# A deformable convolution and a mixture of convolutions on one core: later offset sorting, and other engines for a few copies

## The chip, the core and the metric

The kernel runs on one core of a Trainium2 chip. The metric is the device time of one execution in microseconds. The engines are TensorE (PE; its weight loads are shown as PEld), VectorE (DVE), ScalarE (ACT), GpSimd (POOL) and SyncE (SP). SP, ACT and POOL also issue DMAs; a name with a q (SPq, ACTq) stands for the part of an engine that issues and waits. Each engine takes its instructions in the order in which the program lists them.

## What is computed

The input x has 8 images of 128 channels and 64 x 64 pixels. There are two layers, each of which adds to x. Cut to what matters:

```
gn(v)   : normalise over each group of 4 channels and all pixels of an image
# layer 0: deformable 3 x 3 convolution, then batch norm over all images, ReLU
om      = conv3x3(gn(x), off_w) + off_b          # 27 channels: 9 dy, 9 dx, 9 mask
val[k]  = bilinear sample of gn(x) at (pixel + tap k + (dy, dx)[k]) * sigmoid(mask[k])
y       = sum over k of w[k] applied to val[k] + b
x       = x + relu(batchnorm(y) * gamma + beta)
# layer 1: four expert convolutions, two chosen per image by a gate, and a shared one
x       = x + conv3x3(gn(x), sum of gated experts + shared) + biases
```

The batch norm needs y of all eight images, so layer 1 starts only after layer 0 has done the last one.

## The kernel before

**Sampling as matmuls.** All offsets are below 2 in size (the kernel counts them and has a general path that is not entered here). So a sample is a weighted sum over an 8 x 8 pixel patch. An image is cut into 8 bands of 8 rows, and a band into 15 column tiles, which overlap. For each tile the pixels must stand as patch position by channel. This is the tile `xt`.

- `pick` (VectorE, L768) gathers the 8 even tiles of a band into `picked`, `pixels` has TensorE turn them (L785) in two rounds of four, and ScalarE evicts them (L790).
- `share` (L802) makes the 7 odd tiles from the even ones by eight DMAs of 56 KB within SBUF, because an odd tile is made of the halves of its two even neighbours.

**Weights.** A sample's weights are a product of a y part and an x part with a tent shape. They come from two tables in DRAM for each image, `taby` and `tabx`. For each band, GpSimd issues eight loads of the y part (`load_y`, L719, 90 KB each) and two of the x part (`load_x`, L734, 576 KB each). `spread` turns distances into tents (ScalarE L753 and L756, VectorE L759). `weights` (L825, VectorE) multiplies both into `s`.

**Band loop.** It runs over 64 bands and one more turn. In turn g the five groups of band g are sampled first (`sample`: TensorE L841, eviction ScalarE L851), with `weights` three groups ahead. Then `conv(g - 1)` runs the nine taps of the band before as matmuls on the samples (L890, eviction L898, store of y by SP, L900). Between the taps, by number, stand the preparations for later bands: taps 0 and 1 turn the pixels of band g + 2, tap 2 issues `load_x(g + 3)`, tap 3 issues `share(g + 2)` on SP, tap 4 picks band g + 3, taps 1, 3, 5 and 7 hold the halves of `spread(g + 2)`.

**Tables of the next image.** A generator, `tables(b)`, holds the work that makes the tables of image b, cut into steps. The band loop calls for three steps after each tap (`tick`). A `pause(n)` lets n steps go by, so it says how far along the band loop the next instructions are put. The order in `tables(b)` is:

1. mean and variance by group: matmul pm (L316), d, e, gm on VectorE (L319 to L323), matmul pv (L326), ve (L331), a power on GpSimd (L334), then the normalisation of the image in place
2. the offset convolution, as sums on VectorE (L369, or L419 and L421) and matmuls (L388 or L454), into `om`
3. `om` is stored twice to DRAM, by rows and by columns (L521, L528)
4. both are loaded again, sorted by row (L565, ten DMAs) and by column (L551, five DMAs) into `combo`
5. `distances_y` on VectorE (L608 to L614), sigmoids of the mask (ScalarE L655), then five tents (L633, L637) multiplied by the mask (L670); between the second and the third come L608 again and `distances_x` (L623) and the stores of the x table (L588)
6. the store of the y table (L660)

Between the column loads and step 5 stands the pause that the change touches:

```python
for k, *where in by_column:
    turned_in(nc.sync if b or k == 0 else nc.gpsimd, k, *where)
yield from pause((50, 9)[b] if b < 2 else 17)
```

For images 2 to 7, `tables(b)` starts in image b - 2, in its band 5, and its last steps fall into bands 2 to 4 of image b - 1.

**The start.** Image 0 has no bands to hide behind. Its `tables(0)` runs through before the loop. On the way it picks and turns bands 0 and 1, and near its end, after the first rows of the y table are stored (L660, five DMAs), it issues `share(0)` and `share(1)` on ACT's queue, and two of band 0's eight y loads behind them. Then `tables(1)` is run up to the power on GpSimd, and `dw_sb`, the weights of the taps, is scaled by -1 (L948). Only then come the first three products of `weights`, two on VectorE and one on GpSimd, and the loads of bands 1 and 2.

**Order of the work.** It is written out by hand, there is no scheduler. The DMAs that SP issues get eight completion semaphores in turn: one is not issued before the one eight places earlier has landed.

Of the kernel before, what the change touches and what calls it, by code (L numbers as in the profile page):

```python
# [8 lines left out]
F32 = mybir.dt.float32  # L9
I32 = mybir.dt.int32  # L10
AF = mybir.ActivationFunctionType
# [5 lines left out]
P = 128  # L17
# [24 lines left out]
T = 4  # L42
Q = T + 2 * REACH
HALF = Q * Q
NCOL = 15
# [4 lines left out]
EVEN = (NCOL + 1) // 2  # L50
# [7 lines left out]
BLOCK = "block"  # L58
# [7 lines left out]
def deform_moe_conv(  # L66
# [18 lines left out]
    nc = tc.nc  # L85
# [94 lines left out]
    def dense():  # L180

        with ExitStack() as st:
            st.enter_context(tc.manual_schedule())
            a1 = st.enter_context(tc.tile_pool(name="d1", bufs=1))
# [7 lines left out]


            picked = [a1.tile([P, EVEN, 2, Q, Q], F32, name=f"picked{i}") for i in range(2)]
            for t in pads:
                nc.gpsimd.memset(t[:, 0:ROWPAD], 0.0)
                nc.gpsimd.memset(t[:, ROWPAD + H :], 0.0)
# [11 lines left out]
            ident = a1.tile([P, P], F32, name="ident")  # L209
# [22 lines left out]
            for i, base, mask in ((0, T - REACH, T - 1), (1, 0, Q - 1), (2, T, Q - 1)):  # L232
                one = place_i[:, i : i + 1]
# [36 lines left out]
            def pause(n):  # L270
                for _ in range(n):
                    yield
# [34 lines left out]
            def tables(b):  # L307
# [224 lines left out]
                if b == 0:  # L532
                    for g in range(2):
                        pick(g)
                        for _ in pixels(g):
                            pass
                    pick(2)
                nc.vector.tensor_reduce(
                    most[:, b : b + 1], omr, AX.X, ALU.max, apply_absolute_value=True
                )  # L540
# [30 lines left out]
                    yield from pause(27)  # L571
                for k, *where in by_column:
                    turned_in(nc.sync if b or k == 0 else nc.gpsimd, k, *where)
                yield from pause((50, 9)[b] if b < 2 else 17)

                def moved(side, t, *dims):

# [119 lines left out]
                for i in (3, 0, 4, 1, 2):  # L697
                    masked(i)
                    store_y(i, 1, soon)
                for g in range(2):  # L700
                    share(g, nc.scalar)
                for k in range(2 * T):
                    load_y(0, k, (nc.sync, nc.gpsimd, nc.scalar, nc.gpsimd)[k % 4])
                for _ in statistics(1):
# [7 lines left out]
            def load_y(g, k, engine):  # L712

                if g >= len(bands):
                    return
                b, j = bands[g]
                h, r = divmod(k, T)
                at = HALF * h + r * Q
                engine.dma_start(  # L719
                    out=y_wts[g % 2][at : at + NR * Q, r].rearrange("p a b c -> p (a b c)"),  # L720
                    in_=bass.AP(
                        tensor=y_table[b].tensor,
                        offset=y_table[b].offset + (2 * T * j + k) * GROW,
                        ap=[[YSTEP, NR], [0, Q], [1, YSTEP]],
                    ),
                )
# [34 lines left out]
            def pick(g):  # L761

                if g >= len(bands):
                    return
                b, j = bands[g]
                for h in range(2):
                    one = pads[b % 2][:, 2 * T * j + T * h : 2 * T * j + T * h + 1, 0:1]
                    nc.vector.tensor_copy(  # L768
                        picked[g % 2][:, :, h],
                        bass.AP(  # L770
                            tensor=one.tensor, offset=one.offset,
                            ap=[list(one.ap[0]), [Q, EVEN], [W, Q], [1, Q]],
                        ),
                    )


            def pixels(g):

                if g >= len(bands):
                    return  # L780
                xts[g] = a2.tile([P, NCOL, P], F32, name="xt")
                for c0 in range(0, EVEN, 4):
                    pt = ps_c.tile([P, 4, P], F32, name="pt", tag="pc")
                    for c in range(4):
                        nc.tensor.transpose(  # L785
                            pt[:, c],
                            picked[g % 2][:, c0 + c].rearrange("p h y x -> p (h y x)"),
                            ident,
                        )
                    nc.scalar.copy(xts[g][:, c0 : c0 + 4], pt)  # L790
                    yield


# [1 line left out]
            def share(g, engine):  # L795

                if g >= len(bands):
                    return
                for x0 in range(T):
                    for side in range(2):  # L800
                        rows = slice(x0 + T * side, P, Q)
                        engine.dma_start(  # L802
                            out=xts[g][rows, EVEN:].rearrange("p c n -> p (c n)"),
                            in_=xts[g][rows, 1 - side : EVEN - side].rearrange("p c n -> p (c n)"),
                        )
# [134 lines left out]
                pass  # L940
            for _ in made:
                pass
            for _ in range(2):
                while next(later) != BLOCK:
                    pass
            for _ in range(8):
                next(later)
            nc.scalar.activation(dw_sb, dw_sb, AF.Copy, scale=-1.0)  # L948
            AHEAD = 3
            for n in range(AHEAD):  # L950
                weights(n, nc.vector if n < AHEAD - 1 else nc.gpsimd)
# [33 lines left out]
            for g in range(len(bands) + 1):  # L985
                b, j = bands[g] if g < len(bands) else (B, 0)
                if j == NB - 3:
                    means_of = statistics(b + 2)
                turned = pixels(g + 2)
                if j == NB - 2:  # L990
                    tick()
                for q in range(NGR):
                    if g < len(bands):
                        if g or q + AHEAD < NGR:
                            weights(g * NGR + q + AHEAD)
                        sample(g * NGR + q)
                        if q in (2, 3):
                            for k in range(T * (q - 2), T * (q - 1)):
                                load_y(g + 2, k, nc.gpsimd)
                    if q == 1:  # L1000
                        put_off()
                taps = conv(g - 1) if g else iter(())
                twice = 2 if g and bands[g - 1][1] == NB - 1 else 1
                for done, _ in enumerate(taps):
                    part, odd = divmod(done, twice)
                    if odd == 0 and part in PIXELS:
                        next(turned, None)
                    if odd == 0 and part == 2:
                        load_x(g + 3, nc.gpsimd)
                    if odd == 0 and part in SPREAD:  # L1010
                        step, half = divmod(SPREAD.index(part), 2)
                        if step:
                            spread(g + 2, HALVES[half], ())
                        else:
                            spread(g + 2, sides_=(half,), clip=False)
                    if odd == 0 and part == 3:
                        share(g + 2, nc.sync)
                    if odd == 0 and j == NB - 3 and part in (0, 1, 2, 4):
                        for _ in range(2):
                            next(means_of, None)  # L1020
                    if odd == 0 and j == NB - 3 and part == 7 and b + 2 < B:
                        for _ in made:
                            pass
                        asked, made = True, tables(b + 2)
                        next(made)
                    if odd == 0 and part in BLOCKS and asked:
                        asked = False
                        tick()
                    for _ in range(3 + (g < NB) if twice == 1 else 1 + done % 2):
                        tick()  # L1030
                    if odd == 0 and part == 4:
                        pick(g + 3)
                        if 2 <= j < 5:
                            load_quarter(b + 2, j - 1)
                    if odd == 0 and part == 8 and j == 1:
                        load_quarter(b + 2, 0)
                for _ in turned:
                    pass
                if g == 0:
                    share(2, nc.sync)  # L1040
                    load_x(3, nc.gpsimd)
                    pick(3)
                    spread(1)
                    for n in range(AHEAD):
                        weights(NGR + n)
                    spread(2)
                if g == 4:
                    quad_weights()
                if g < len(bands):
                    late.append((close, g))  # L1050
                xts.pop(g - 1, None)
                if j == 1 and b:
                    nc.vector.bn_aggr(ymvs[:, b - 1], ystats[:, b - 1])
                if (b, j) == (B - 1, 1):
                    reach()
# [596 lines left out]
```

## Time and profile before

| what | us |
|---|---|
| median of 3 runs | 1505.06 (1503.42 to 1509.43) |
| the profiled execution | 1515.66 |
| its span, first to last instruction | 1513.9 |
| first sampling matmul (L841) | 83.55 |
| TensorE busy | 1311.9 |
| VectorE busy | 960.6 |
| ScalarE busy | 784.5 |
| GpSimd busy | 442.2 |

The mean granted clock of TensorE is 0.935 of the full one. Each image takes about 129 us in the middle of layer 0 (its last band's taps start at 514.36 us for image 2 and at 643.09 us for image 3). The sampling ends at about 1140 us, then layer 1 follows.

The profile's page gives busy times, a chain of waits that ended last, and groups of instructions by line. The timeline shows instructions in order of time with the idle time of the engine before each. A stall of TensorE in this kernel is read in three steps: find the gap, see which engine released it, and see in that engine's own timeline what it had stood at.

### The profile page before, as it was taken

What the parts mean: (1) busy time and instruction counts of PE and PEld (TensorE: products, weight loads), DVE (VectorE), ACT (ScalarE), POOL (GpSimd) and SP (SyncE); (2) the same over time, 40 slices, a digit from 0 to 9 for tenths busy, and PEclk for the clock granted to TensorE, in tenths of its full rate; (3) what the DMA queues carried; (4) which work ended last, traced back from release to release, by engine and by line L of the source; (5) the groups of instructions that cost most, each with busy time, mean ns of one, the idle gap of its engine ahead of it and who ended that gap; (6) DMA issues with size and microseconds to landing.
All of it is one profiled execution on the core that took longest, in us unless ns stands there. A gap on an engine that the chain in (4) does not pass through costs nothing.

```text
span 1513.9 us, 22086 instructions
## 1 busy us (share of the span) xinstructions
PE 1311.9 (87%) x7554; PEld 751.2 (50%) x7554; DVE 960.6 (63%) x1985; ACT 784.5 (52%) x1055; POOL 442.2 (29%) x751
## 2 busy tenths in 40 slices
PE   4049788889979997997998899798994999999998
PEld 1033455655645664564665556466652444444443
DVE  5436477548746855864784786544427888888872
ACT  2144674666657675665757566664634232323320
POOL 6242332333324242343433434343403000110100
PEclk9569989989989998998999899899996999999999
DMA  4476774898689788779969987798927345555411
GB/s 144 107 150 161 177 180 110 184 233 205 164 197 219 180 190 210 196 175 210 218 167 196 222 209 182 169 216 205 236 62 230 90 133 162 166 165 155 111 43 58
DMA packets 136670, 256.71 MB, mean 170 GB/s; under 512 B 81554, under 2 KB 84782, under 8 KB 127862
## 3 DMA queue, kind: packets, MB, share of 16 engines
q0 software_dynamic: 55344, 137.45, 41.6%
q1 hardware_dynamic: 80532, 116.45, 27.4%
q10 hardware_dynamic: 674, 1.32, 0.3%
q8 instruction: 62, 1.02, 0.3%
q14 instruction: 58, 0.48, 0.1%
HBM read 180.23 MB, written 45.35 MB: 149 GB/s over the span
## 4 chain that ended last, share of the span: by engine, by line
PE 47%; DMA 24%; DVE 12%; issue 8%; SPq 4%; ACT 3%; POOL 2%; DVEq 0%; POOLq 0%; ACTq 0%
PE pc L1564 17%; PE py L890 15%; PE pq L841 9%; DMA xt<-xt 7%; DMA xwts<-tabx 4%; DMA combo<-colwise 3%; DMA combo<-rowwise 3%; DMA pad<-in_x_dram 3%; PE pc L454 2%; PE pt L785 2%; DMA ywts<-taby 2%; SPq L565 2%; DVE combo L421 2%; DVE s L825 2%; DVE xwts L759 1%
## 5 line engine op out<-in xcount | busy, mean ns | idle before, releaser
L890 PE MATMUL py<-samples,dw_sb 128*128 128x512 f32 (+3 forms) x1296 | 556.4, 564 | 8.0 <-ACT y L898 6.2
L719 POOL DMA_DIRECT2D ywts<-taby x508 | 295.7, 607 | 557.0 <-DVE s L825 483.8
L841 PE MATMUL pq<-s,xt 64*128 64x144 f32 (+1 forms) x3840 | 303.2, 313 | 94.0 <-DVE s L825 67.9
L841 PEld LDWEIGHTS pq<-s,xt 64*128 64x128 f32 x3840 | 273.0, 201 | 139.4 <-issue 97.5
L851 ACT COPY samples<-pq 128x864 f32<-128x864 f32 (+1 forms) x320 | 284.7, 972 | 109.9 <-PE pq L841 108.8
L890 PEld LDWEIGHTS py<-samples,dw_sb 128*128 128x128 f32 x1296 | 230.3, 191 | 208.6 <-issue 179.0
L825 DVE TENSOR_TENSOR s<-xwts,ywts 128x72 f32<-128x72 f32 (+1 forms) x447 | 199.5, 499 | 73.6 <-PE pq L841 65.6
L759 DVE TENSOR_SCALAR xwts<-xwts 128x1152 f32<-128x1152 f32 (+2 forms) x128 | 92.5, 755 | 175.3 <-ACT xwts L753 134.0
L1564 PE MATMUL pc<-v,u 128*128 128x512 f32 x384 | 175.7, 604 | 6.6 <-DVE v L1471 6.4
L1564 PE MATMUL pc<-v,wmix 128*128 128x512 f32 x384 | 173.1, 596 | 0.0
L753 ACT ACTIVATE xwts<-xwts,place 128x1152 f32<-128x1152 f32 (+3 forms) x132 | 152.9, 1162 | 31.0 <-DMA xwts<-tabx 31.0
L1542 ACT ACTIVATE t<-pc,bmix 128x512 f32<-128x512 f32 x32 | 22.0, 687 | 188.9 <-PE pc L1564 100.3
L1564 PEld LDWEIGHTS pc<-v,u 128*128 128x128 f32 x384 | 72.4, 192 | 94.3 <-issue 84.2
L1564 PEld LDWEIGHTS pc<-v,wmix 128*128 128x128 f32 x384 | 71.9, 189 | 90.6 <-issue 88.7
L790 ACT COPY xt<-pt 128x512 f32<-128x512 f32 x128 | 74.8, 584 | 62.6 <-PE pt L785 56.1
L898 ACT ACTIVATE y<-py,db_sb 128x512 f32<-128x512 f32 (+3 forms) x72 | 45.7, 635 | 116.0 <-PE py L890 72.3
L785 PEld LDWEIGHTS pt<-ident,picked 128*128 128x128 f32 x512 | 60.2, 142 | 77.3 <-ACT xt L790 39.8
L734 POOL DMA_DIRECT2D xwts<-tabx x128 | 75.0, 597 | 71.4 <-DMA ywts<-taby 31.9
L785 PE MATMUL pt<-ident,picked 128*128 128x128 f32 x512 | 80.5, 280 | 5.1 <-ACT xt L790 3.1
L670 DVE TENSOR_TENSOR work<-work,combo 64x576 f32<-64x576 f32 x40 | 29.6, 749 | 68.1 <-ACT work L637 68.1
L976 DVE BATCH_NORM_STATS2 ystats<-y 128x6 f32<-128x512 f32 (+3 forms) x72 | 44.4, 625 | 20.0 <-ACT y L898 20.0
L768 DVE COPY picked<-pad 128x512 f32<-128x512 f32 x128 | 48.3, 419 | 1.5 <-PE pt L785 1.5
(200 smaller groups left out, 1070.8 us busy)
## 6 DMA issues: line engine op xcount, KB each, us to landing
xwts<-tabx POOLq DMA_DIRECT2D x128, 576.0 KB, 8.7
ywts<-taby POOLq DMA_DIRECT2D x508, 90.0 KB, 5.4
xt<-xt SPq DMA_DIRECT2D x496, 56.0 KB
pad<-in_x_dram SPq DMA_DIRECT2D x36, 512.0 KB
out_dram<-yo SPq DMA_DIRECT2D x32, 512.0 KB
yd<-y SPq DMA_DIRECT2D x48, 256.0 KB
pad<-yd SPq DMA_DIRECT2D x16, 512.0 KB
x<-yd SPq DMA_DIRECT2D x16, 512.0 KB
```

The lines of the kernel that those rows point to most:

```text
L719: engine.dma_start(out=y_wts[g % 2][at : at + NR * Q, r].rearrange("p a b c -> p (a b c)"), in_=bass.AP(tensor=y_table[b].tensor, offset=y ...
L734: engine.dma_start(out=x_wts[g % 3][HALF * h : HALF * h + HALF], in_=bass.AP(tensor=x_table[b].tensor, offset=x_table[b].offset + (2 * j + ...
L753: nc.scalar.activation(some, some, AF.Abs, bias=columns[side])
L759: nc.vector.tensor_scalar(some, some, -1.0, 0.0, ALU.add, ALU.min)
L768: nc.vector.tensor_copy(picked[g % 2][:, :, h], bass.AP(tensor=one.tensor, offset=one.offset, ap=[list(one.ap[0]), [Q, EVEN], [W, Q], [1, Q]],
L785: nc.tensor.transpose(pt[:, c], picked[g % 2][:, c0 + c].rearrange("p h y x -> p (h y x)"), ident,)
L790: nc.scalar.copy(xts[g][:, c0 : c0 + 4], pt)
L825: engine.tensor_tensor(s[:, :, 3 * at : 3 * (at + k)].rearrange("p m (c x) -> p m c x", x=3), by_x[:, :, c : c + k], by_y[:, :, w : w + k] ...
L841: nc.tensor.matmul(by_m[:, h, :, at : at + k], lhsT=xts[g][rows, c // 2 + EVEN * (c % 2)], rhs=s[rows, :, at : at + k], start=True, stop=True,
L851: nc.scalar.copy(bass.AP(tensor=one.tensor, offset=one.offset + first, ap=[list(one.ap[0]), [M * PLANE, 2], [PLANE, M], [WB + 1, 3], [1, w ...
L890: nc.tensor.matmul(py, lhsT=dw_sb[:, 3 * (2 - yy) + 2 - xx], rhs=samples[g % 2][:, m : m + 3 * n - 2 : 3, xx, 1 : W + 1], start=(i == 0), ...
L1564: nc.tensor.matmul(pc, lhsT=us[j][:, kx], rhs=vs[g][:, rows, kx : kx + W], start=(kx == 0), stop=(kx == 2),)
```

## The change

It has five edits.

1. Band 0's odd tiles: two VectorE copies build `picked_odd`, and `pixels` turns 15 tiles instead of 8, in four rounds instead of two. `share(0)` is not called any more.
2. `share(1)` goes from ACT's queue to SP's, between the column loads of `tables(0)` and the stores of the y table.
3. The beginning of `tables(1)` goes from before the loop to turn 0, after the second group of samples. The scaling of `dw_sb` goes into `tables(0)`, behind the turned pixels.
4. The pause before step 5 is 35 steps instead of 17 for images 2 to 7.
5. `share(5)`, in turn 3, is issued by GpSimd instead of SP.

```diff
                 if b == 0:
                     for g in range(2):
                         pick(g)
-                        for _ in pixels(g):
+                        for _ in pixels(g, turn_odd=not g):
                             pass
                     pick(2)
+                    nc.scalar.activation(dw_sb, dw_sb, AF.Copy, scale=-1.0)
...
-                yield from pause((50, 9)[b] if b < 2 else 17)
+                if b == 0:
+                    share(1, nc.sync)
+                yield from pause((50, 9)[b] if b < 2 else 35)
...
-                for g in range(2):
-                    share(g, nc.scalar)
...
-            def pixels(g):
+            def pixels(g, turn_odd=False):
...
-                for c0 in range(0, EVEN, 4):
+                if turn_odd:
+                    for side in range(2):
+                        nc.vector.tensor_copy(
+                            picked_odd[:, :, :, :, T * side : T * side + T].rearrange(
+                                "p c h y x -> p c (h y) x"
+                            ),
+                            picked[g % 2][
+                                :, 1 - side : EVEN - side, :, :, T * side : T * side + T
+                            ].rearrange("p c h y x -> p c (h y) x"),
+                        )
+                for c0 in range(0, NCOL if turn_odd else EVEN, 4):
+                    n = min(4, NCOL - c0)
...
-            for _ in range(2):
-                while next(later) != BLOCK:
-                    pass
-            for _ in range(8):
-                next(later)
-            nc.scalar.activation(dw_sb, dw_sb, AF.Copy, scale=-1.0)
...
+                    if g == 0 and q == 1:
+                        for _ in range(2):
+                            while next(later) != BLOCK:
+                                pass
+                        for _ in range(8):
+                            next(later)
...
-                        share(g + 2, nc.sync)
+                        share(g + 2, nc.gpsimd if g == 3 else nc.sync)
```

## The prediction

> **What bounds the kernel now.** I read in this order: busy shares, chain of waits, TensorE's timeline for its gaps, and for each gap the timelines of VectorE, SyncE, ScalarE and GpSimd.
>
> ```profile
> PE 1311.9 (87%) x7554; PEld 751.2 (50%) x7554; DVE 960.6 (63%) x1985; ACT 784.5 (52%) x1055; POOL 442.2 (29%) x751
> PE 47%; DMA 24%; DVE 12%; issue 8%; SPq 4%; ACT 3%; POOL 2%; DVEq 0%; POOLq 0%; ACTq 0%
> ```
>
> TensorE is busy for 87%, but only 47% of the chain is its own: the rest are places where it stands still. The change touches three kinds.
>
> The start, where TensorE first samples at 83.55 us (timeline rows: start and duration in us, engine, line, operation, count; in brackets the idle time before and what ended it):
>
> ```profile
> 50.63 24.10 ACTq L802 DMA_DIRECT2D xt<-xt  x16
> 76.52 0.41 ACT L756 ACTIVATE xwts<-xwts,place 128x144 f32<-128x144 f32 x1 [25.22 <-DMA xt<-xt]
> 81.76 2.77 DVE L825 TENSOR_TENSOR s<-xwts,ywts 128x432 f32<-128x432 f32 x4
> ```
>
> ScalarE's queue spends 24.10 us issuing the 16 copies of bands 0 and 1; only then can it spread band 0's weights.
>
> The fifth band of image 0:
>
> ```profile
> 159.82 10.64 SPq L802 DMA_DIRECT2D xt<-xt  x8
> 170.51 6.25 SPq L565 DMA_DIRECT2D combo<-rowwise  x10
> 182.14 0.31 DVE L608 TENSOR_SCALAR combo<-combo,nudge 64x192 f32<-64x192 f32 x1 [11.88 <-DMA combo<-rowwise]
> 190.95 3.49 PE L841 MATMUL pq<-s,xt 64*128 64x144 f32 x24 [9.90 <-ACT samples L851]
> ```
>
> SyncE issues eight copies before the offset loads L565; VectorE, in order, stands 11.88 us at L608, TensorE 9.90 us behind it.
>
> Once per image, here in image 4:
>
> ```profile
> 692.12 8.48 SPq L551 DMA_DIRECT2D combo<-colwise  x5
> 703.92 4.96 SPq L802 DMA_DIRECT2D xt<-xt  x8
> 705.97 0.56 DVE L608 TENSOR_SCALAR combo<-combo,nudge 64x192 f32<-64x192 f32 x2 [7.77 <-DMA combo<-colwise]
> 709.79 3.49 PE L841 MATMUL pq<-s,xt 64*128 64x144 f32 x24 [8.81 <-DVE s L825]
> 753.26 1.87 PE L841 MATMUL pq<-s,xt 64*128 64x144 f32 x24 [0.38 <-DVE s L825]
> ```
>
> VectorE reaches the x half of L608 before the column loads L551 have landed; the sample weights L825 are queued behind, and TensorE loses 8.81 us. The same 24 matmuls take 1.87 us where no long gap came before.
>
> [...] 3.49 against 1.87 us after the gap, and the next two taps 2.07 against 1.15. A gap costs about 2.5 us beyond itself. [...]
>
> **Part 1, the start.** Removed: 16 issues on ScalarE (24.10). Added: two VectorE copies of 448 elements (a pick of 512 takes 0.42: 0.8 together), seven transposes (0.66 to 1.1 per four) and two evictions (0.58 each). The transpose and eviction rounds now end at 40.9 and take 1.3 to 1.8 each, so two more end at about 44; the dw scaling (1.15, now at 79.75 beside VectorE) follows, to 45.3. Cover: ScalarE's sigmoids start at 45.96, held by the column loads. Without cover, up to 2 us. Eight copies move to SyncE, behind L551 (ends 44.80), ahead of the five table stores L660 (first at 52.89). Eight cost 5.0 usually, 10.6 at worst in the quoted rows: ending at 50 or 55.4, cost 0 to 2.5. I take 0; the others vanish, which also frees the DMA engines.
>
> What is late next is the weights' load: GpSimd's L588 is released by its first half at 62.87, so both halves are in at about 65; the y rows, last issued at 60.4 on GpSimd with 5.4 us to landing, at about 66. ScalarE's two own y loads move from 74.77 to about 60. From spread to first product was 5.24 us, of which 1.3 are the second image's mean (d, e, gm, then ve waiting on TensorE). So products start at 65.5 + 3.9 = 69.4 instead of 81.76: **12 us** (9 to 13). Band 1's loads, issued from 83.35 right behind GpSimd's product, shift with it.
>
> The mean's remainder goes after group 1: pm and pv (0.6 each) now stand between samples, pv waiting for e behind VectorE's fifth product: at most 1 us, and TensorE then waits 7.08 for band 1's weights anyway. Its pow waits in GpSimd behind load_x(2), which ends at 97.5; the reader is at 113.9. I take 0, at most 1.
>
> **Part 2, band 5's copies.** Without the eight issues L565 starts once the row stores (issued to 155.8) have landed. In image 0 L565 followed their last issue by 3.3 us (34.3 to 37.54); here, with the column stores issued to 159.5, I take 161 (159.6 to 164) instead of 170.51. VectorE's wait falls from 11.88 to about 2.4, its products come at 180 instead of 189.4, and TensorE is free for them at 181.05. Gain 9.9 plus the cold clock 2.5, less 1.9: **10.5 us** (6 to 12.4). On GpSimd the eight issues stand between load_x(6), ended 159.2, and load_y(6), 167.47: idle now. At 0.57 each (its y loads: 4.54 for eight) they take 4.6; should the last two wait until L734 lands (8.7 after 157.9), load_y is 1 us late, a band ahead of its reader. No row shows this copy on GpSimd; between 0 and 2.
>
> **Part 3, 18 steps.** A tap gives three steps, so everything from distances_y on moves by six of nine taps, in images 1 to 6 (tables 2 to 7). Moved: L608 to L670, the tents on ScalarE, and the stores L588 and L660, which go behind the next band's eight copies on SyncE, L588 for table 2 behind the present band's. No arithmetic changes.
>
> For tables 3 to 7 TensorE's gaps are 6.90, 8.65, 8.81, 8.91, 7.85, sum 41.1; with 2.5 of cold clock each, 53.6. After the move VectorE reaches the x half at tap 3 of the next band, about 705 in the rows above, where the loads land at 705.97. The gap goes.
>
> Late next are the copies. Those of the following band are issued 703.92 to 708.88. The preceding eight, issued to 692.1, released TensorE at 698.75, some 6.5 later, so these are in at about 713 to 715; with the gap gone TensorE wants them at 697.4 + 4.2 (samples) + 0.7 (the wait at 698.75) + 9.0 (taps) = 711.3. The DMA engines, 77% busy in that stretch and up to 107% before it, will be fuller. I give back 3.3 us per image (0 to 8): 53.6 - 16.5 = 37. For table 2 the gap is of this very kind:
>
> ```profile
> 334.39 6.60 PE L841 MATMUL pq<-s,xt 64*128 64x144 f32 x56 [6.56 <-DMA pad<-in_x_dram]
> ```
>
> There L588 (310.39, 5.00) and its neighbours stand ahead of the copies at 320.83, and the change takes L588 out of their way. Of 9.2 (6.56 and cold clock 2.7) I take 5 (0 to 9). Part 3: **42 us** (10 to 62).
>
> Do the tables still arrive? SyncE: copies to 708.9, x and yd to 710, next copies to 716, L588 to 718, landed 2.1 later (the first tabx store's time on the chain) at 720; load_x of the next image stands at 718.5. Another eight copies from 719.5 to 724.5, L660 at 725, landed 728; load_y (4.6 of issue, 5.4 of landing) is in at 738. VectorE reaches its first product at 740, TensorE needs it at 751.
>
> **Sum.** 12 + 10.5 + 42 = 64.5 off the profiled execution's 1515.66 us gives 1451. That execution is 10.6 above the median of the runs, 1505.06, so I take the saving from the median: 1440.6, and state **1442 us**, since residual waits are more often forgotten than counted twice.
>
> **Rivals.**
> Copies late (0.27): the SyncE queue, not VectorE, holds the image; the gap comes back one band later as a wait for xt. For it: 24% DMA on the chain, 7.3% xt<-xt, and 334.39. Against: SyncE idles from 712.6 on. Part 3 is then 0 to 20: 1505 - 22.5 - 10 = 1472 (1462 to 1484).
> Start and band 5 fail (0.05): the copies on SyncE hold L660, or GpSimd's copies hold its loads. Only part 3: 1463.
> Tables late (0.05, slower): SyncE's backlog grows, L660 misses its slack of 751 - 738 = 13 us, GpSimd's queue stands at load_y, and the first band of the next image waits. Each us beyond 13 costs six times, once per image; the 65 us are eaten at 13 + 11 = 24 us late, from there it is slower. At 26 late: 1442 + 6 x 13 = 1520. Against it: SyncE issues nothing from 712.6 to 717.9.
> The change does nothing (0.03): the waits only shift by six taps. In the changed program L588 and L660 do stand behind those copies on SyncE, and L608 behind another band's products, so it acts.
>
> **Numbers.** 0.60 for the forecast, whose own span is 1420 to 1462. The range 1420 to 1482 reaches into "copies late". Half a percent, 7.5 us, is about what a measurement of this kernel tells from no change: faster 0.92, same 0.03, slower 0.05.
>
> **What would show it.** Right: first sample near 71 us; no L608 wait above 3 us on VectorE (52 us over the colwise and rowwise rows now); the gap near 191 gone; the last taps of image 1 to 6 without a [.. <-DVE s] gap above 5 us. Wrong: new TensorE gaps on xt<-xt or on POOL ywts at an image's first band, copies issued over more than 8 us, or load_x waiting on tabx.

## The result, and the profile after

The median went from 1505.09 us (22 runs) to 1491.97 us (22 runs), ratio 0.9902 with a 95% interval of 0.9877 to 0.9927: 13.1 us faster, where the prediction had 63. The ratio leaves out three slow runs of the changed kernel, over 1.5% above its fastest, and so stands for 14.8 us. The two profiled executions lie further apart than the medians: the one of before, 1515.66 us, is 10.6 above its median, the one of after, 1483.92 us, 8 below. So traces are used below for where time goes, medians for how much. Lines have moved: sampling L841 is now L853, weights L825 is L837, copies L802 L814, column loads L551 L553, sorting L608 L612, x table stores L588 L592, y table stores L660 L664, the mean's matmul pm L316 L317.

The page's busy times and the chain's shares by engine, after:

```profile
PE 1312.5 (89%) x7561; PEld 750.7 (51%) x7561; DVE 961.2 (65%) x1987; ACT 786.3 (53%) x1057; POOL 450.7 (30%) x759
PE 44%; DMA 26%; DVE 12%; issue 8%; SPq 5%; ACT 3%; POOL 1%; DVEq 0%; POOLq 0%; ACTq 0%
```

No engine does less. The chain is less TensorE's own than before (44% against 47%) and more DMA's and SyncE's.

The start, after (timeline rows of ScalarE and TensorE):

```profile
57.65 1.62 ACTq L721 DMA_DIRECT2D ywts<-taby  x2
64.69 0.41 ACT L758 ACTIVATE xwts<-xwts,place 128x144 f32<-128x144 f32 x1 [13.04 <-DMA xwts<-tabx]
71.24 3.49 PE L853 MATMUL pq<-s,xt 64*128 64x216 f32 x24 [27.73 <-DVE s L837]
```

ScalarE issues no copies any more, spreads at 64.69 instead of 76.52, and TensorE samples 12.3 us sooner.

Band 5 of image 0, after (rows of TensorE, VectorE, TensorE):

```profile
167.41 1.94 PE L853 MATMUL pq<-s,xt 64*128 64x144 f32 x24 [2.05 <-ACT samples L863]
178.42 0.56 DVE L612 TENSOR_SCALAR combo<-combo,nudge 64x192 f32<-64x192 f32 x2 [6.33 <-DMA combo<-colwise]
185.69 0.56 PE L317 MATMUL pm<-mv,gsel 128*128 128x1 f32 x2 [8.25 <-DVE mv L305]
```

The gap of 9.90 us is down to 2.05. But VectorE now stands at the x half of the same sorting, statistics are queued behind it, and TensorE waits 8.25 us for their mean in the same turn.

Image 4, after (rows of SyncE, then of VectorE and TensorE):

```profile
664.61 10.71 SPq L553 DMA_DIRECT2D combo<-colwise  x5
...
676.42 8.23 SPq L814 DMA_DIRECT2D xt<-xt  x8
684.75 0.53 SPq L280 DMA_DIRECT2D pad<-in_x_dram  x1
...
685.84 8.84 SPq L814 DMA_DIRECT2D xt<-xt  x8
695.04 2.55 SPq L592 DMA_DIRECT2D tabx<-combo  x6
697.70 0.41 SPq L280 DMA_DIRECT2D pad<-in_x_dram  x1
```

```profile
681.02 0.56 DVE L612 TENSOR_SCALAR combo<-combo,nudge 64x192 f32<-64x192 f32 x2
...
691.52 6.04 PE L853 MATMUL pq<-s,xt 64*128 64x144 f32 x56 [7.25 <-DMA yd<-y]
...
705.42 1.28 DVE L302 BATCH_NORM_STATS2 stats<-pad 128x6 f32<-128x512 f32 x2 [2.36 <-DMA pad<-in_x_dram]
707.25 0.35 PE L317 MATMUL pm<-mv,gsel 128*128 128x1 f32 x2 [1.60 <-DVE mv L305]
```

L612 no longer waits, as forecast. TensorE stops one band later instead. At 691.52 it is released by a DMA. The one named is a store of y, but sampling reads only `s` and `xt`. The eight semaphores that this matmul waits for are those of the copies issued from 676.42, the last of which landed at 691.38, while the store landed at 693.01; so it waited for the copies. Then comes a short wait for pm, behind statistics of a quarter of the next-but-one image that was issued at 697.70, behind the x table stores.

The sampling starts in both traces give the sum. A turn lasts from its first sampling matmul to that of the next turn; turn 4 is the one that samples band 4 (before to after, us):

| image | turn 4 | turn 5 | turn 6 |
|---|---|---|---|
| 2 | 26.3 to 14.2 | 13.9 to 22.1 | 13.1 to 13.7 |
| 3 | 25.7 to 14.1 | 13.8 to 23.4 | 13.1 to 15.3 |
| 4 | 25.9 to 14.3 | 13.8 to 26.1 | 13.1 to 14.8 |
| 5 | 24.8 to 13.3 | 14.2 to 24.7 | 13.1 to 13.1 |
| 6 | 23.3 to 13.3 | 13.2 to 14.0 | 13.1 to 13.1 |

In images 2 to 5, 46.8 us left turn 4, and about 45 came back in turns 5 and 6. In turn 5 of images 2 and 3 the wait for the mean is the longer one (5.22 and 4.39 us at pm), in images 4 and 5 that for the copies (7.25 and 6.43). In image 1, whose stall stood in turn 5, that turn lost 9.6 us and turn 4 grew by 7.6. In image 6 the gain stayed, but the first turn of image 7 then grew from 21.4 to 25.0.

Busy time by stretch, after, in image 4 (turns 3, 4 and 5; the last three columns are granted clock, share of the DMA engines, GB/s):

```profile
core 0: us, PE busy (x) PEld busy (x) DVE busy (x) ACT busy (x) POOL busy (x), PEclk, DMA share, GB/s
656.10:669.40 13.30, 13.30 (x89) 7.96 (x88) 7.39 (x19) 10.33 (x15) 5.80 (x10) 1.00 1.09 233
669.40:683.60 14.20, 13.31 (x87) 7.75 (x86) 8.41 (x22) 13.08 (x19) 5.64 (x10) 1.00 0.98 207
683.60:709.70 26.10, 16.41 (x91) 10.45 (x90) 15.38 (x32) 11.42 (x15) 5.64 (x10) 0.87 0.85 213
```

The DMA engines are full in turns 3 and 4 (shares of 1.09 and 0.98), in which TensorE runs almost without a gap. Over the image's eight turns the shares times the lengths make about 112 us of 130. TensorE is busy for 119 us there, so the DMA engines have little slack beside it.

### The profile page after: what moved, and what is told of

It is laid out like the page before. It is cut to its first block, busy times and chain, and to the rows that moved or that the text cites. A ratio compares the mean times of both kernels' runs of the same rounds, so it can differ in the third digit from the quotient of the medians.

```text
span 1482.1 us, 22076 instructions
## 1 busy us (share of the span) xinstructions
PE 1312.5 (89%) x7561; PEld 750.7 (51%) x7561; DVE 961.2 (65%) x1987; ACT 786.3 (53%) x1057; POOL 450.7 (30%) x759
## 4 chain that ended last, share of the span: by engine, by line
PE 44%; DMA 26%; DVE 12%; issue 8%; SPq 5%; ACT 3%; POOL 1%; DVEq 0%; POOLq 0%; ACTq 0%
PE py L902 15%; PE pc L1576 13%; PE pq L853 10%; DMA xt<-xt 10%; DMA pad<-in_x_dram 5%; DMA combo<-rowwise 4%; PE pc L455 2%; DMA yd<-y 2%; PE pt L799 2%; SPq L814 2%; DMA ywts<-taby 2%; SPq L567 2%; DVE combo L422 2%; DMA x<-in_x_dram 1%; DVE s L837 1%
## 5 line engine op out<-in xcount | busy, mean ns | idle before, releaser
L853 PE MATMUL pq<-s,xt 64*128 64x144 f32 (+1 forms) x3840 | 301.4, 313 | 79.1 <-DVE s L837 48.0
L853 PEld LDWEIGHTS pq<-s,xt 64*128 64x128 f32 x3840 | 272.7, 201 | 124.5 <-issue 45.3
L837 DVE TENSOR_TENSOR s<-xwts,ywts 128x72 f32<-128x72 f32 (+1 forms) x447 | 200.6, 500 | 89.9 <-PE pq L853 76.8
L802 ACT COPY xt<-pt 128x512 f32<-128x512 f32 (+1 forms) x130 | 75.9, 584 | 59.8 <-PE pt L799 55.8
L302 DVE BATCH_NORM_STATS2 stats<-pad 128x6 f32<-128x512 f32 x64 | 39.7, 826 | 14.7 <-DMA pad<-in_x_dram 14.7
```

Source lines behind the costliest of these rows:

```text
L802: nc.scalar.copy(xts[g][:, c0 : c0 + n], pt[:, 0:n])
L837: engine.tensor_tensor(s[:, :, 3 * at : 3 * (at + k)].rearrange("p m (c x) -> p m c x", x=3), by_x[:, :, c : c + k], by_y[:, :, w : w + k] ...
L853: nc.tensor.matmul(by_m[:, h, :, at : at + k], lhsT=xts[g][rows, c // 2 + EVEN * (c % 2)], rhs=s[rows, :, at : at + k], start=True, stop=True,
```

## The experiments

"Before" is 1504.5 to 1507.6 us in the four groups; each ratio is to the "before" of its own group.

**The parts, each by itself.** Edits 1 to 3 alone; edit 5 alone; edit 4 alone; all but edit 4.

```diff
# e_start = after with: pause 17, share(g + 2, nc.sync)
# e_pool  = before with:
-                        share(g + 2, nc.sync)
+                        share(g + 2, nc.gpsimd if g == 3 else nc.sync)
# e_pause = before with 17 -> 35;  e_nopause = after with 35 -> 17
```

> The kernel before with edits 1, 2 and 3 alone (the start). Theory A, the prediction's sizes: 12 us faster than before. Theory B, from the trace after: the first sample comes 12.3 us earlier and bands 1 and 2 another 3.5, so 15 to 16 us faster, which would be more than the whole change brought (13.1); the other two parts together would then bring nothing or cost 2 to 3 us. First sampling matmul near 71 us in both.

> The kernel before with edit 5 alone (band 5's copies issued by GpSimd). Theory A: 10.5 us faster, the gap near 191 us falls from 9.90 to about 2 us. Theory B: the gap falls, but VectorE now stands at the x half of L608 and TensorE meets a new wait on the mean of the image after next (pm, L316) about 20 us later: 3 to 4 us faster.

> The kernel before with edit 4 alone (pause of 35 steps). Theory A: 42 us faster. Theory B: the VectorE gap in the band before the last of each image goes, and waits for xt and for pm come in the last band of the same image instead: 0 to 14 us faster (the running offset between the two traces changes by 13.6 us over images 1 to 7, of which 9 in image 6 alone). Theory C, the later sorting costs in itself because stores and copies collide: up to 5 us slower.

> The changed kernel without edit 4 (pause back to 17). Theory A: 42 us slower than the changed kernel, 22 faster than before. Theory B: about 19 us faster than before by the offset that the traces show at the end of image 0, so 0 to 6 us faster than the changed kernel if edit 4 brings nothing, or up to 14 slower than it if edit 4 brings what the offset shows.

| kernel | median us | ratio, 95% | at 1505 us |
|---|---|---|---|
| e_start | 1496.09 | 0.9927 (0.9903 to 0.9950) | -11.0 |
| e_pool | 1500.47 | 0.9952 (0.9933 to 0.9972) | -7.2 |
| e_pause | 1516.03 | 1.0051 (1.0026 to 1.0077) | +7.7 |
| e_nopause | 1490.33 | 0.9884 (0.9859 to 0.9909) | -17.5 |

The start brings what was forecast for it, the copies of band 5 about two thirds (7.2 of 10.5 us), and the two add up: 18.2, with 17.5 measured together. Edit 4 alone makes the kernel slower. Only theory C allowed a loss, of up to 5 us; the measured 7.7 lies above that, and its interval (3.9 to 11.6) just reaches into it. (In the later groups theory C is another one, on the DMA engines.) The three parts sum to -10.5, and all of them measured -14.8 by ratio (-18.5 to -11.0), and since the sum carries the errors of three runs, no joint effect is resolved. On top of the other edits, edit 4 makes no difference that can be resolved: 0.9902 with it and 0.9884 without it, 2.7 us apart, with intervals that overlap. The profiled execution of e_pause (1503.5 us) is the fastest of its 11, so its trace understates the loss.

**Is it SyncE's queue or the DMA engines?** The copies for bands 4 and 5 by GpSimd (q_after); half the bytes of each x load, with and without edit 4 (l_after, l_nopause; the other half of the weights then keeps old values, so these kernels don't compute the layer and only price the bytes); no copies for band 5, its odd tiles turned by TensorE (o_after). Theory Q takes the queue for the cause, theory C the DMA engines.

```diff
# q_after
+  share(g + 2, nc.gpsimd if g == 3 or (8 < g < 56 and g % 8 in (2, 3)) else nc.sync)
# l_after; l_nopause has pause 17 besides
+                n = XROW // 2 if 8 < g < 56 else XROW
-                        out=x_wts[g % 3][HALF * h : HALF * h + HALF],
+                        out=x_wts[g % 3][HALF * h : HALF * h + HALF, :n],
-                            ap=[[0, HALF], [1, XROW]],
+                            ap=[[0, HALF], [1, n]],
# o_after
+                odd_by_pe = 8 < g < 56 and g % 8 == 3
+                turned = pixels(g + 2, turn_odd=odd_by_pe)
-                    if odd == 0 and part == 3:
+                    if odd == 0 and part == 3 and not odd_by_pe:
```

> The changed kernel with one more edit: the copies issued in turns 2 and 3 of images 1 to 6 (for bands 4 and 5, which follow the column loads) go through GpSimd's queue instead of SyncE's. The same bytes, another queue. Theory Q (SyncE's queue holds the copies back: eight take 8.2 to 8.8 us to issue behind the column loads where they take 5.0 elsewhere): the waits of 5 to 7 us for xt in band 5 go, 20 to 40 us faster than the changed kernel, 1450 to 1475. Theory C (the DMA engines are at their limit, with a share of 0.85 over the whole image and 0.98 to 1.09 in its first bands): the copies land no sooner, within 6 us of the changed kernel's 1492, or slower, since GpSimd's loads of the y part now stand behind copies.

> The changed kernel without edit 4, and with each load of the x part (load_x) cut to half its bytes in images 1 to 6; the number of DMAs and their places stay. The other half of the weights then holds old values. In the trace these loads keep the DMA engines busy for about 42 us per image, so 21 us per image fall away. Theory C (DMA engines): each image loses 4 to 10 us of TensorE's waits, 25 to 60 us faster than without edit 4 at full loads (1490). Theory Q (the queue's order): within 10 us of 1490.

> The changed kernel with each load of the x part cut to half its bytes in images 1 to 6, as in the one before, with edit 4 in. Theory C: with room on the DMA engines nothing is late next when VectorE's wait goes, so that this comes near TensorE's own 117 us per image, 1430 to 1445, and is 5 to 40 us faster than the one without edit 4. Theory Q: the copies stay behind the column loads on SyncE, 1475 to 1495, and edit 4 brings nothing here either.

> The changed kernel with band 5's odd tiles turned by TensorE in images 1 to 6, so that no copies are made for it. Costs about 1.2 us of TensorE and 1.2 us of ScalarE per image, and two VectorE copies of 0.4 us. Theory Q and theory C both take the copies for late: the waits for xt in band 5 go. If those were the only ones, 25 to 40 us faster than the changed kernel (1452 to 1467). If the load of pad and with it the mean of the image after next (pm) is late behind them, as the trace after has it in images 1, 2 and 3 (4.4 to 8 us), only 0 to 15 us faster (1477 to 1492).

Measured: q_after 1477.35 us (0.9815, 0.9778 to 0.9853), o_after 1478.04 (0.9799, 0.9764 to 0.9833), l_nopause 1437.74 (0.9552, 0.9513 to 0.9592), l_after 1447.57 (0.9589, 0.9555 to 0.9623). Fewer bytes on GpSimd's loads, which are in another queue, take 53 and 44 us away. For l_nopause that is within theory C's range, l_after ends 3 us above its own, and theory Q fails for both. Yet moving the same bytes to another queue brought about 15 us, more than theory C's 6 and less than theory Q's 20 to 40. So both hold a part. In o_after the waits for band 5's copies are gone from images 2 to 6, but pm waits 4.06 to 6.50 us in images 2 to 5, and the time is in the second of its two ranges. How the two queues share the DMA engines no run shows. The issue times on SyncE did come down when GpSimd's loads became lighter: the eight copies right behind the column loads took 8.23 to 11.62 us to issue in images 2 to 5 of the changed kernel (8.23 at 676.42 above) and 4.97 to 9.85 us in l_after at half x loads.

And l_after lost to l_nopause by 10 us by the medians (by the ratios 6, with intervals that overlap), though no wait for copies was left in its trace. SyncE, VectorE and TensorE in l_after, image 4 (its lines stand one lower from L734 on):

```profile
657.88 8.19 SPq L815 DMA_DIRECT2D xt<-xt  x8
666.17 4.83 SPq L592 DMA_DIRECT2D tabx<-combo  x6
671.10 0.40 SPq L280 DMA_DIRECT2D pad<-in_x_dram  x1
```

```profile
678.73 1.29 DVE L302 BATCH_NORM_STATS2 stats<-pad 128x6 f32<-128x512 f32 x2 [4.35 <-DMA pad<-in_x_dram]
...
680.57 0.56 PE L317 MATMUL pm<-mv,gsel 128*128 128x1 f32 x2 [4.05 <-DVE mv L305]
```

This is a wait that edit 4 itself made. It put the six x table stores from ahead of a turn's copies to behind them, right in front of the load of pad's last quarter (pad holds the image whose statistics are taken). That load is what the statistics wait for, and pm, in order on TensorE, for them.

**Other places, and the copies ahead of the column loads.** o_after with 41 steps, which puts the stores behind that load (o41); 26 steps (p26); without edit 4, copies by GpSimd (q_nopause); without edit 4, band 4's odd tiles turned by TensorE (o2_nopause), so that no copies stand ahead of the column loads.

```diff
# o41 = o_after with 35 -> 41;  p26 = after with 35 -> 26;  q_nopause = q_after with 35 -> 17
# o2_nopause = after with 35 -> 17 and
+                odd_by_pe = 8 < g < 56 and g % 8 == 2
+                turned = pixels(g + 2, turn_odd=odd_by_pe)
+                    if odd == 0 and part == 3 and not odd_by_pe:
```

> The changed kernel with band 5's odd tiles turned by TensorE in images 1 to 6 and with a pause of 41 steps instead of 35. The six steps put the stores of the x table (L592) behind the load of the last quarter of pad on SyncE's queue; otherwise little moves. With 35 steps that load stands behind six stores (4.8 us of issue) and behind eight copies, and the mean of the image after next (pm) waits 4.1 to 6.5 us for it in images 2 to 5, cold clock apart. Theory M (edit 4 put the stores ahead of that load, and this is what was late next): these waits fall to under 2 us, 15 to 30 us faster than with 35 steps (1478): 1448 to 1463. Theory C (the DMA engines are full and the quarter lands late in any place): within 6 us of 1478. In both, the tables of the next image come about 2 us later, which may cost up to 15 us at the images' first bands.

> The changed kernel without edit 4, and with band 4's odd tiles turned by TensorE in images 1 to 6. Its eight copies, which stand ahead of the column loads on SyncE's queue (8.6 us of issue in the trace without edit 4), are gone, so the column loads are issued about 8 us sooner and VectorE's wait at the x half (7 to 9.6 us) should go without anything being put later. Cost about 1.2 us of TensorE per image. If the order on the queue was the cause of that wait: 30 to 45 us faster than without edit 4 (1490), 1445 to 1460. If the DMA engines hold the column loads back anyway: 1475 to 1495.

> The changed kernel with a pause of 26 steps, half way between 17 (1490) and 35 (1492). The x half of the sorting goes to tap 0 of band 4's turn, the stores of the x table stand ahead of the copies of that turn. If waits are only passed on from one place to the next, this is 1485 to 1495 as both ends are. If between the two ends VectorE's wait for the column loads is short and the load of pad's last quarter isn't yet behind the stores, 1465 to 1480.

> The changed kernel without edit 4, and with the copies of turns 2 and 3 of images 1 to 6 issued by GpSimd. With edit 4 the same move gave 1477 where SyncE's queue gave 1492. SyncE's column loads start about 8 us sooner. Theory Q: VectorE's wait goes, 1450 to 1465, faster than with edit 4, since the stores stay ahead of the load of pad. Theory C: the DMA engines carry the same bytes in the same stretch, 1475 to 1490.

Measured: o41 1471.39 us (0.9788, 0.9748 to 0.9827), o2_nopause 1454.68 (0.9683, 0.9647 to 0.9718), p26 1511.77 (1.0039, 1.0013 to 1.0065), q_nopause 1476.12 (0.9821, 0.9776 to 0.9865).

p26 missed both expectations: half way is 20 us worse than either end. SyncE, VectorE and TensorE in p26, image 4:

```profile
703.39 7.02 SPq L592 DMA_DIRECT2D tabx<-combo  x6
711.99 5.21 SPq L814 DMA_DIRECT2D xt<-xt  x8
717.30 0.52 SPq L280 DMA_DIRECT2D pad<-in_x_dram  x1
```

```profile
710.22 5.84 PE L853 MATMUL pq<-s,xt 64*128 64x144 f32 x56 [8.52 <-DMA yd<-y]
...
728.17 1.29 DVE L302 BATCH_NORM_STATS2 stats<-pad 128x6 f32<-128x512 f32 x2 [8.76 <-DMA pad<-in_x_dram]
...
730.01 0.56 PE L317 MATMUL pm<-mv,gsel 128*128 128x1 f32 x2 [5.85 <-DVE mv L305]
```

TensorE first waits for band 5's copies, as with 35 steps. Then the mean is late: the stores take 7.02 us to issue, and with them in front the turn's copies and the last quarter of pad both come later, so that VectorE stands 8.76 us for that quarter. With 17 steps the order on SyncE is the same, but the stores were issued in 2.21 us before the copies were due (image 4 of e_nopause), and in that trace the mean is on time. So the time is not a smooth function of the pause. That the fuller queue makes the difference between these two is read from their traces; no run changed it alone.

o2_nopause is the fastest version that computes the layers: by the medians 50 us faster than before and 36 faster than e_nopause, which differs by its one edit (48 and 30 by the ratios). With no copies ahead of them, the column loads go out at once, and the sorting stays where it was (SyncE, VectorE, TensorE; image 4; the last line is TensorE's at the same place in e_nopause):

```profile
643.62 7.80 SPq L553 DMA_DIRECT2D combo<-colwise  x5
```

```profile
660.69 0.56 DVE L612 TENSOR_SCALAR combo<-combo,nudge 64x192 f32<-64x192 f32 x2
...
664.55 1.87 PE L853 MATMUL pq<-s,xt 64*128 64x144 f32 x24 [2.11 <-DVE s L837]
...
687.59 0.28 PE L317 MATMUL pm<-mv,gsel 128*128 128x1 f32 x2
...
684.92 3.49 PE L853 MATMUL pq<-s,xt 64*128 64x144 f32 x24 [7.50 <-DVE s L837]
```

No wait at L612, a gap of 2.11 us instead of 7.50, and pm waits for nothing: with 17 steps the stores don't stand right in front of the last quarter. Theory C's 1475 to 1495 fails here, but that the order on SyncE's queue was enough is not shown, since the eight copies are gone altogether. q_nopause also takes the copies out from in front of the column loads and keeps all bytes, on GpSimd's queue. It brought 14 us instead of 36 and fell into theory C's range. In its trace the gap at the sorting shrinks as well, to 2.10 to 2.83 us in images 2 to 6, but turn 5 then lasts 15.8 to 22.2 us in images 2 to 5, where e_nopause has 13.9. Whether the bytes or the order on GpSimd's queue keep the rest back stays open.

o41 does not settle its question by time: its interval overlaps that of o_after. In its trace pm's wait is under 1 us in images 3 and 4, but still 3.40 and 2.51 us in images 2 and 5.

**What edit 4 costs where nothing else is late.** l_after with 41 steps (l_41); o2_nopause with edit 4 put back (o2_after); o2_nopause with band 5 of image 0 by TensorE as well, instead of edit 5 (o2_plus: `odd_by_pe = g == 3 or ...`).

> The changed kernel with each load of the x part cut to half its bytes in images 1 to 6, and with a pause of 41 steps, so that the stores of the x table stand behind the load of pad's last quarter on SyncE. At these light loads 35 steps gave 1448 and 17 steps 1438, and the trace with 35 steps has no wait for copies left, but one of 2.4 to 4.4 us for the mean (pm) in images 2 to 5. Theory M (that wait is what edit 4 costs): 1433 to 1441, the pm waits gone. If the tables' lateness at the first band of an image is the cost (the y table's stores are later still with 41 steps): 1448 to 1456.

> The changed kernel, edit 4 in, with band 4's odd tiles turned by TensorE in images 1 to 6. Without edit 4 the same gave 1455. If edit 4 only moves a wait that is now gone, it can only cost here, by the mean's wait behind the stores (4 to 6 us of wait and cold clock in each of images 2 to 5, and the late y table in image 6): 1470 to 1485. If it still spared VectorE a wait, 1445 to 1455.

> The changed kernel without edit 4, with band 4's odd tiles turned by TensorE in images 1 to 6 and band 5's in image 0 too, in place of the copies by GpSimd (edit 5). Eight copies fewer on the DMA engines in image 0, and GpSimd's load of the x part that waited there 11 us is free. If DMA work was what held band 5's turn: 2 to 6 us faster than 1455. If that turn is held by the order on VectorE (the x half of L608 ahead of the statistics): 1452 to 1458, no difference that can be measured.

Measured: l_41 1442.59 us (0.9570, 0.9544 to 0.9596), o2_after 1469.79 (0.9756, 0.9727 to 0.9786), o2_plus 1457.64 (0.9671, 0.9635 to 0.9708). SyncE and TensorE in l_41, image 4:

```profile
665.37 0.34 SPq L280 DMA_DIRECT2D pad<-in_x_dram  x1
665.81 2.84 SPq L592 DMA_DIRECT2D tabx<-combo  x6
```

```profile
677.32 0.35 PE L317 MATMUL pm<-mv,gsel 128*128 128x1 f32 x2 [0.74 <-DVE mv L305]
```

With the stores behind the quarter, pm's wait falls from 4.05 to 0.74. The median lies between those of l_nopause and l_after, 5 us from each, outside both expected ranges, and the intervals do not separate it from either. The traces split the cost: band 0 of image 7 is first sampled at 941.9 us without edit 4, at 948.9 with 35 steps, at 942.4 with 41; that turn then lasts 15.3, 22.1 and 24.4 us. So 35 steps cost about 7 us up to there, which 41 steps give back, and both cost 7 to 9 us at the entry into image 7. There the y table is late: GpSimd waits 12.20 and 13.37 us for it before it can load band 0's y part (l_after, l_41); l_nopause has no such wait. The changed kernel has the same at full loads (GpSimd's timeline, end of image 6):

```profile
964.07 5.07 POOL L721 DMA_DIRECT2D ywts<-taby  x8 [10.65 <-DMA taby<-work]
```

The trace of before has no such wait. At the ends of images 2 to 5 of the changed kernel GpSimd stands 5.43 to 6.12 us for the table as well, but there the first turn of the next image is no longer than before. o2_after against o2_nopause prices edit 4 where its stall is gone: the ratios differ by 0.0073, 11 us of loss (15 by the medians), and the intervals do not overlap. Its trace has pm waiting 1.73 to 3.93 us in images 2 to 5. o2_plus is not to be told from o2_nopause by time. In its trace pm waits 1.27 us in band 5's turn of image 0 instead of 5.38, so with those copies gone the statistics there come sooner.

## Why the prediction was right or wrong

**Part 1, 12 us (9 to 13): right.** e_start measured 11.0 (7.5 to 14.6). First sample at 71.24, forecast near 71. In the traces band 2 came 3.5 us sooner on top, which I had not counted.

**Part 2, 10.5 us (6 to 12.4): right in range, high in size.** e_pool measured 7.2 (4.2 to 10.1). The gap near 191 fell to 2.05, as worked out. The missing term is the one that stands behind it: I followed the row loads, L612's first half and the weights, but not the second half of L612 and the statistics queued behind it, whose mean TensorE takes in order in the same turn. That wait is 8.25 us here and 5.58 us in e_pool, and the turn got only 3.5 and 5.8 us shorter in the two traces.

**Part 3, 42 us (10 to 62): wrong, and in sign.** The first half of the step holds: the gap goes, in all five images. The step that failed is "I give back 3.3 us per image (0 to 8)". The traces show 11.3 per image in images 2 to 5, and e_pause, 7.7 us slower, shows that by the ratio all of it and more comes back. Three things were missing in it.

1. The size of what I had seen. I let the column loads take 8.48 us and the copies 4.96 us on SyncE, as before, and had the copies in 2 to 4 us late. After, the same two take 10.71 and 8.23 us in image 4, 5.5 more together, and TensorE waits 7.25 us, with the cold clock after it (the 56 matmuls at 691.52 take 6.04 us, where 56 of the same kind take 3.83 at 670.89; the clock's records show half the full one from 689.2 to 696.1). The short times had been read inside the stall that the edit removes: in images 2 to 5 the copies right behind the column loads take 4.96 to 5.83 us before and 8.23 to 11.62 after. SyncE's idle time from 712.6 on, which was held against the rival, is of the same kind: it comes right after the stall. "The DMA engines, 77% busy in that stretch and up to 107% before it, will be fuller" stood in the text without a price. At half the x loads no wait for copies is left: shown.
2. "The stores L588 and L660, which go behind the next band's eight copies on SyncE": I followed them on to load_x and load_y on GpSimd, but did not look at what they would now stand in front of on SyncE itself, the load of pad's last quarter, nor at its readers. With the stores behind it, pm's wait goes: shown by the traces. That it is about half of what edit 4 costs at light loads rests on medians that the intervals do not separate.
3. "L660 at 725, landed 728; load_y [...] is in at 738", against a need at 751, was worked out for image 4 and taken for all. At the end of image 6 GpSimd stands 10.65 us for the table, and the first turn of image 7 grows by 3.6 us.

The rival "copies late" (0.27) had the mechanism, but its price, a gain of 0 to 20 us for part 3, left no room for a loss. "Tables late" came true in part: GpSimd waited at five images, TensorE's time grew at one. The sum of 64.5 thus became 11.0 + 7.2 - 7.7 = 10.5, with 13.1 measured by the medians. The measured 1492 lies above the stated range, whose upper end, 1482, was to take in late copies. The sign of the whole was right only by parts 1 and 2.

## What to carry to other kernels

In this kernel a stall of the busiest engine was also time in which queues and DMA engines caught up: eight copies took 4.96 to 5.83 us to issue inside it, and 8.23 to 11.62 once it was gone. Before a stall is booked as a gain, add up the DMA share over the whole period (here 112 us of 130, beside 119 of the engine's own work): here most of the gap returned at the next transfer. This is a warning and not a bound, since the sum moves with the schedule: o2_nopause does image 4 in 120 us, with a sum of 104. And before an operation is put later to dodge a late load, look at what makes the load late: making the eight copies in front of it needless brought 30 to 36 us, putting its reader later cost 8 by itself.

## What the runs showed of the hardware that was not expected

The time that eight equal copies take to issue is no property of the copy. On SyncE it was 4.97 us in image 4 of l_after, 8.23 at the same place in the changed kernel, 11.93 in p26 (at 719.55) and 14.43 in o_after (at 551.17). What the queue waits for, the landing of the DMA eight places before, stands in the chain of the changed kernel, in the middle of the copies from 676.42:

```profile
675.42 8.10 DMA pad<-in_x_dram
683.52 0.02 issue
683.53 0.49 SPq L814
```

The seventh copy goes out at 683.53, when the load of pad, issued eight places earlier at 675.42, has landed.

The cold clock, half the full one in the records, does not follow every short gap either. After gaps of 2.1 us before the same 24 matmuls, they took 1.87 us in o2_nopause's images 4, 5 and 6, 2.21 us in image 3 and 3.38 us in image 2. The records of the granted clock in the traces tell these apart. In all 17 traces the clock changes only at the ends of slots of 3.41 us, on a grid that stays fixed through a run. There are 6461 slots at full clock. By the profile's matmul times, every one in which TensorE was idle for 2.0 us or more was followed by half the clock, and none in which it was idle for less than 1.1 us; between the two figures both happen. The gap in image 2 lay within one slot. Those in images 4, 5 and 6 were cut by the end of a slot, so that at most 1.87, 1.15 and 1.16 us fell into one.
